# Six tile buffers in the room of the turned ones, masks in two fixed places, and new planning times

## The chip, the cores and the metric

The kernel runs on one core of one Trainium2 chip. The metric is the device time of one execution in microseconds. Time before: 2075.99 us, the median of 3 runs (2071.98 to 2077.3).

## The reference

Two graph layers over N = 3327 nodes with 256 features, all in float32. `adj` is dense in storage, with about 0.5% of its entries above zero.

```python
def _top_p_attention(X, W1, W2, W3):
    q = X @ W1.T @ W2.T
    k = X @ W3.T
    probs = softmax(q @ k.T)
    idx = argsort(-probs)
    sp = take_along_axis(probs, idx)
    cs = cumsum(sp)
    keep_sorted = cs - sp < 0.9
    mask = zeros.at[rows, idx].set(keep_sorted)
    A = probs * mask
    return A / A.sum(-1, keepdims=True)

def layer0(X, S):                       # S = adj, X = relu(layernorm(x))
    R = S + eye(N); R = R / R.sum(-1, keepdims=True)
    Z, Xf, Xa = 0, X, X
    for n in range(2):
        A = _top_p_attention(Xa, W1, W2, W3)
        Xf = R @ Xf
        Xa = A @ Xa
        Z = Z + Xf @ U1[n].T + Xa @ U2[n].T
    return layernorm(X + Z) * ln_g + ln_b

def layer1(h, adj):                     # h = relu(layernorm(x)), 4 heads of 64
    hp = (h @ W).reshape(n, 4, 64)
    s, d = hp . a_src, hp . a_dst
    e = leaky_relu(s[:, :, None] + d[:, None, :], 0.2)
    e = where(adj > 0, e, -inf)
    attn = softmax(e, axis=2)
    return elu(einsum('hij,jhf->ihf', attn, hp))

x = x + layer0(relu(layernorm(x)), adj)
x = x + layer1(relu(layernorm(x)), adj)
```

## The kernel before

Nodes are cut into NT = 26 tiles of 128. The work has three stages. In the two steps of layer 0 (n = 0 and 1 in the code, step 1 and step 2 in the text), each of 26 rows of tiles goes through an attention chain, and each tile also has a full product R @ Xf. Layer 1 then runs over four blocks b of 832 target nodes, with j over the 26 source tiles.

**Who decides the order.** All work is given to a planner (`Plan`, L471 to L583) as pieces: an engine, an estimated length, a rank, the pieces that it needs, and named buffers that it takes and gives back. `order` plays the pieces through in time: whenever an engine is free, it takes the ready piece of lowest rank whose buffers are free. `lag` is the time that the plan lets pass between the end of a piece and the moment when another engine may use its result. The outcome is one fixed order of instructions on each engine. On the chip each engine works its queue in order and waits on semaphores; the plan's times have no other effect than this order. SP (SyncE) issues nearly all DMAs, in one queue.

**A row of attention** (`search` and `attention`, L1463 to L1538). TensorE (PE) makes the logits into `pl` (L906), ScalarE (ACT) exponentiates them into one of the buffers `e` (L921), and ACT and GpSimd (POOL) find a threshold in 2 or 3 evaluations (`count` L958, `step`). VectorE (DVE) takes candidates (`window` L1016 and L1021), sorts, and drops what is below the threshold (`drop` L1072). The row is then transposed: DVE transposes inside 32x32 blocks (`turn_blocks` L1084), SP writes one of three groups to the array `blocks` in HBM (`put_blocks` L1088) and reads it back in the other order in four DMAs (`get_blocks` L1093). PE multiplies its 26 blocks (`attend_blocks` L1100) into the accumulator `acca`, ACT takes the result out (`attended` L1104), and the row's buffer `e` is free. A float32 matmul shows in the profile as two records.

**A full product** (`Full`, L1109, and `full`, L1540). Seven loads of four 128x128 tiles of adj each (256 KB, L1119) go into the buffers `at`; POOL adds the identity to the diagonal tile (`diagonal` L1132); PE multiplies (`some` L1125) into the accumulator `accf`. In step 1 the result is copied to a buffer `f` (`copy` L1136 or `take` L1146), from which DVE adds it (`add`, L1152); in step 2 it is scaled into `main` (L1139 or L1142). Full products are what PE does while rows are not ready. Step 2's need all of step 1's.

**The `stats` of four rows** (L811 to L865): PE makes a product, ACT copies it out of PSUM (`copy` L828), and DVE squares and sums it (L833), ahead of the rows' thresholds.

**Layer 1** (`attend_neighbours`, L1565). For each j two loads (256 and 192 KB, L1680) bring adj's tiles into `at`; ACT makes a mask of zeros and ones from them (Relu L1690, Sign L1691); DVE makes the masked exponents of four heads (L1702, four instructions a j); PE multiplies them (`product` L1718) and sums them (`sums` L1732). The `sums` use the accumulators `acca` and `accf`, so the first of them waits until the last row is `attended`. For j = 0 and 1 of the first block the tiles come into a room of their own (`load_first` L1667) and their masks lie in two places of the scratch buffer `junk` (L1675). The targets' exponents are broadcast from HBM to all partitions once for each block (`broadcast`, L1634). At a block's end the result goes through PSUM, a nonlinearity and the addition of x1, which is fetched into a buffer `f` (L1824), and is stored (L1888).

**Buffers.** The pool `apool` holds `at` (4 of 2 KB a partition), `etpool` holds `et` (3 of 2 KB), used for the masks of layer 1, for the copies of `stats` and for two weights; `f` has 3 buffers of 1056 bytes. The plan counts them as `at=4`, `et=3`, `mask=2`, `f=3` (L867 and L54). Their planning times:

```python
b = plan.put("SP", 0.5, rank - 1.0, row.put_blocks, g, needs=[b], lag=8.0)          # L1527
[plan.put("SP", 0.6, rank - 1.0, row.get_blocks, g, o, needs=[b], lag=5.5) ...]     # L1530
plan.put("SP", 0.4, rank, f.load, q, needs=[after], take=["at"], lag=4.0)           # L1544
full(n, t, (2.0 + 1.3 * t if n == 0 else base + 1.0 + t), ...)                      # L1969
```

`base` is 30 in step 2; row i has the rank base + i, with small offsets for its pieces.

Of the kernel before, what the change touches and what calls it, by code (L numbers as in the profile page):

```python
# [10 lines left out]
F32 = mybir.dt.float32  # L11
BF16 = mybir.dt.bfloat16
# [7 lines left out]
P = 128  # L20
# [5 lines left out]
H = 4  # L26
# [24 lines left out]

REACH = 40.0

BUFS = dict(kk=2, e=4, sc=6, f=3, xa=2, xt=2, kq=3, ystage=2, base=1, mv=4, cum=2)  # L54


@with_exitstack
# [529 lines left out]
def fast(  # L587
# [58 lines left out]
    with ExitStack() as l0:  # L646
        wpool = l0.enter_context(tc.tile_pool(name="wpool", bufs=1))
        small = l0.enter_context(tc.tile_pool(name="small", bufs=2))
        epool = l0.enter_context(tc.tile_pool(name="epool", bufs=4))
        apool = l0.enter_context(tc.tile_pool(name="apool", bufs=4))  # L650
        etpool = l0.enter_context(tc.tile_pool(name="etpool", bufs=3))
        scr = l0.enter_context(tc.tile_pool(name="scr", bufs=1))
        ps_l = l0.enter_context(tc.tile_pool(name="ps_l", bufs=2, space=PSUM))
        ps_a = l0.enter_context(tc.tile_pool(name="ps_a", bufs=1, space=PSUM))
# [20 lines left out]
            GP.memset(gk, 0.0)  # L675
            GP.tensor_copy(gk[:DA, DA + 1 :], ident[:DA, :DA])

        small.tile([P, 8], F32, name="room", bufs=1)
        stat = wpool.tile([P, 2, NT], F32, name="stat")
        sig, zadd, cn, cs = (wpool.tile([P, NT], F32, name=n) for n in ("sig", "zadd", "cn", "cs"))  # L680
        met = wpool.tile([P, 6, NT], F32, name="met")
# [17 lines left out]

        def weights():  # L700
            held = {}
            w1 = etpool.tile([P, 4, P], F32, name="et")
            w1 = w1[:, 0, :].rearrange("p (c o) -> p c o", c=2)
            w2 = small.tile([P, PIECES, 8], F32, name="cands").rearrange("p c r -> p (c r)")[:DA, :DA]
            w1r = small.tile([P, PIECES * 8], F32, name="rest", bufs=1)[:DA].rearrange("p (k o) -> p k o", k=1)
            w1r = [w1r[:, 0, :], small.tile([P, P], F32, name="kq", bufs=BUFS["kq"])[:DA]]
            nc.scalar.dma_start(w1, w1t.rearrange("(c p) o -> p c o", p=P))
            nc.scalar.dma_start(w2, w2t)
            for r in range(2):
                nc.scalar.dma_start(wqk[:, :, r, r * DA : r * DA + DA], w3t.rearrange("(c p) o -> p c o", p=P))  # L710
            for n in range(STEPS):
                cols = slice((1 - n) * D, (2 - n) * D)
                uloads.append(
                    plan.put(
                        "SP", 0.4, -196.5 + n, nc.sync.dma_start, u1[:, :, cols],
                        u1t[n].rearrange("(c p) o -> p c o", p=P), lag=8.0,
                    )
                )

            S.activation(adds[:, 2:], powers[:, :1], AF.Exp)  # L720

            def turn():
                held["ps"] = ps_x.tile([DA, 2, P], F32, name="px")
                for k in range(2):
                    T.transpose(held["ps"][:, k, :], w1[:, k, :], ident)

            def copy():
                for k in range(2):
                    S.copy(w1r[k], held["ps"][:, k, :])

            def product():
                held["ps"] = ps_x.tile([P, 2, DA], F32, name="px")
                for k in range(2):
                    T.matmul(held["ps"][:, k, :], w1r[k], w2, start=True, stop=True)

            def place():
                for r in range(2):
                    S.copy(wqk[:, :, r, (1 - r) * DA : (2 - r) * DA], held["ps"])

            a = plan.put("PE", 0.25, -200.0, turn, take=["px"], needs=[plan.put("", 0.0, -201.0, lambda: None, lag=8.0)])  # L740
            a = plan.put("ACT", 0.5, -200.0, copy, needs=[a], take=["kq"], give=["px"])
            a = plan.put("PE", 0.25, -200.0, product, needs=[a], take=["px"], give=["kq"])
            return plan.put("ACT", 0.5, -200.0, place, needs=[a], give=["px"])
# [8 lines left out]
        def layer1_loads():  # L752

            late = wpool.tile([P, 2 * D + 2 * (H * FH + 2 * H)], F32, name="late")
            g_all, b_all = late[:, :D], late[:, D : 2 * D]
            wa = late[:, 2 * D :].rearrange("p (c o) -> p c o", c=2)
            a_all = etpool.tile([P, H, 2 * FH], F32, name="et")
            nc.sync.dma_start(g_all, ln_g.partition_broadcast(P))
            nc.sync.dma_start(b_all, ln_b.partition_broadcast(P))
            nc.sync.dma_start(a_all, gat_a.partition_broadcast(P))  # L760
            nc.sync.dma_start(wa[:, :, : H * FH], gat_w.rearrange("(c p) o -> p c o", p=P))
            return g_all, b_all, wa, a_all

        def layer1_scores(wa, a_all):

            prod = etpool.tile([P, 2, H, FH], F32, name="et")
            for k in range(2):
                for a in range(2):
                    V.tensor_mul(
                        prod[:, 0],  # L770
                        wa[:, k, : H * FH].rearrange("p (h f) -> p h f", h=H),
                        a_all[:, :, a * FH : (a + 1) * FH],
                    )
                    lo = H * FH + a * H
                    V.tensor_reduce(wa[:, k, lo : lo + H], prod[:, 0], AX.X, ALU.add)

        def moments(n, t, kq, ps_k, ps_g):

# [32 lines left out]
        def stats(n, lo, hi, rank, needs, scaled):  # L811
# [11 lines left out]
                    T.matmul(held["ps"][:, k, :], qg[n, t0 // 4][:, at, :], gks[n], start=True, stop=True)  # L823

            def copy(held, m):
                qg = etpool.tile([P, 4, P], F32, name="et").rearrange("p a b -> p (a b)")
                held["qg"] = qg[:, : 3 * (2 * DA + 1)].rearrange("p (a b) -> p a b", a=3)
                S.copy(held["qg"][:, :m, :], held["ps"][:, :m, :])  # L828

            def square(held, t0, m):  # L830
# [8 lines left out]
            for t0 in range(lo, hi, 2):  # L839
                held, m = {}, min(2, hi - t0)  # L840
                a = plan.put("PE", 0.25 * m, rank, product, held, t0, m, needs=[needs, scaled], take=["px"])
                a = plan.put("ACT", 0.45, rank, copy, held, m, needs=[a], take=["et"], give=["px"])
                ends.append(plan.put("DVE", 0.35 * m + 0.2, rank, square, held, t0, m, needs=[a], give=["et"]))

            def variance():
                V.tensor_mul(cn[:, s], mu, mu)
# [17 lines left out]
            a = plan.put("ACT", 0.6, rank, exps, needs=[a])  # L864
            return plan.put("DVE", 0.6, rank, rest, needs=[a]), ends  # L865

        plan = Plan(dict(rows=1, mvs=3, pl=2, px=2, acca=1, accf=1, et=3, at=4, y=1, e2=2, ec=1, mask=2, e5=1, qg=2, **BUFS))  # L867
        own_e = [[("e", "e5")[i % 5 == 2 - n] for i in range(NT)] for n in range(STEPS)]
        qg = {}

# [649 lines left out]
        def attention(row, rank, total, drops, right):  # L1520
            a = None
            come = []
            for g in range(3):
                b = plan.put(
                    "DVE", 1.17 if g < 2 else 1.44, rank - 1.001, row.turn_blocks, g, needs=[drops[g]]
                )
                b = plan.put("SP", 0.5, rank - 1.0, row.put_blocks, g, needs=[b], lag=8.0)  # L1527
                b = plan.put("", 0.0, -90.0, lambda: None, needs=[b], lag=0.0)
                come.append(
                    [plan.put("SP", 0.6, rank - 1.0, row.get_blocks, g, o, needs=[b], lag=5.5) for o in range(4)]  # L1530
                )
            for j in range(0, NT - 2, 4):
                js = range(j, j + 4 if j < 20 else NT)
# [6 lines left out]
        def full(n, t, rank, right, after):  # L1540

            f = Full(n, t)
            loads = [
                plan.put("SP", 0.4, rank, f.load, q, needs=[after], take=["at"], lag=4.0) for q in range(-(-NT // JC))  # L1544
            ]
            loaded[0] = loads[-1]
            a, own = None, plan.put("POOL", 0.4, -90.0, f.diagonal, needs=[loads[t // JC]])
# [17 lines left out]
        def attend_neighbours(rows, ends, done, fulls):  # L1565
# [80 lines left out]
            for b in range(4):  # L1646
# [9 lines left out]
                def open_den(q=q):  # L1656
                    q["den"] = [ps_a.tile([P, 512], F32, name=n) for n in ("acca", "accf")]

                seen, last_acc, last_den, last_e = [], None, None, None
                group, halves = [], [None, None]  # L1660
                for j in range(NT):
                    rank = r0 + 9.0 * j / NT if b > 0 or j >= 2 else 54.2 + 0.1 * j
# [18 lines left out]
                            at[:, : len(ts), :], adjt[ts[0] : ts[0] + len(ts), :, j, :].rearrange("i p q -> p i q")  # L1681
                        )

                    def mask(held=held, off=off):
                        m = etpool.tile([P, 4, P], F32, name="et").rearrange("p a b -> p (a b)").bitcast(BF16)
                        m = held["mask"] = m[:, :W]
                        A, B = (held.pop(g).rearrange("p i q -> p (i q)") for g in range(2))
                        A, B = A[:, off:], B[:, : W + off - 4 * P]
                        for to, src in ((m[:, : 4 * P - off], A), (m[:, 4 * P - off :], B)):
# [48 lines left out]
                                    tile_position=(0, 32 * k),  # L1738
                                )

                    own = ["et", "mask"]
                    if b == 0 and j < 2:
                        loads, own = plan.put("SP", 0.2, rank, load_first, needs=[opened[0]], lag=4.0), []
                        m_ = plan.put("ACT", 1.8, rank, mask_first, needs=[loads])
                    else:
                        loads = [
                            plan.put("SP", 0.4, rank, load, g, needs=[logits_done], take=["at"], lag=4.0)
                            for g in range(2)
                        ]
                        m_ = plan.put("ACT", 2.2, rank, mask, needs=[loads], take=own, give=["at", "at"])  # L1750
                    mine = ("e", "e", "e", "ec", "e", "e2", "e2")[j % 7]
                    x_ = plan.put(
                        "DVE", 2.0, rank, exponents, 0, needs=[m_, both[0], ends[j][0], dict(ec=opened, e2=more).get(mine),
# [189 lines left out]
        for n in range(STEPS):  # L1943
# [22 lines left out]
            if n == 0:  # L1966
                drawn[0] = rows[-1].pieces["logits"]
            fulls = [
                full(n, t, (2.0 + 1.3 * t if n == 0 else base + 1.0 + t), [p[0] for p in sources], [p[1] for p in sources] if n == 0 else loaded[0])  # L1969
                for t in range(NT)  # L1970
            ]
            done = [attention(r, base + r.i, *found[r.i], right) for r in rows]
# [1 line left out]
            if n == 0:  # L1974
# [21 lines left out]
                def layer1():  # L1996
# [4 lines left out]
                a = plan.put("SP", 1.8, base + NT + 1.0, layer1, needs=[used, stored], take=["et"], lag=8.0)  # L2001
                less = plan.put("POOL", 0.6, base + 5.0, lambda: late["less"](), needs=[a])
                layer1_ready = plan.put(
                    "DVE", 3.7, base + 5.0, lambda: layer1_scores(late["wa"], late["a"]), needs=[a], take=["et"],
                    give=["et", "et"],
                )
                layer1_ready = [layer1_ready, less]
            else:
# [72 lines left out]
```

## Time and profile before

| | |
|---|---|
| median of the runs | 2075.99 us |
| the profiled execution | 2077.04 us |
| its span, first to last instruction | 2075.2 us |
| mean granted TensorE clock | 0.992 |
| VectorE busy | 1696.3 us (82%) |
| ScalarE busy | 1298.7 us (63%) |
| bytes moved by DMA | 361.61 MB, mean 174 GB/s |

The span in 40 slices of 52 us; a digit is the busy share in tenths:

```profile
PE   8999999999999999999999999999998999999997
DVE  5479989887997742888679888898888999999894
ACT  4677685677756405884677777877643456474642
PEclk9999999999999999999999999999999999999999
DMA  3177677776786756687757777676786444444440
```

Step 1 ends near slice 15 (about 780 us), where DVE and ACT nearly stop: step 2's keys need the last row of step 1. Step 2 ends near slice 31 (about 1600 us), and layer 1 follows, where DVE is as full as PE.

The costliest groups of instructions on PE (columns: line, engine, operation, out<-in, shapes, count, busy us, mean ns, idle us before them and what ended it):

```profile
L1100 PE MATMUL acca<-rhs,e 128*128 128x256 f32 x2184 | 485.6, 380 | 4.1 <-DMA e<-blocks 2.3
L1125 PE MATMUL accf<-main,at 128*128 128x257 f32 x1352 | 323.8, 389 | 14.1 <-DMA at<-in_adjt_dram 7.6
L1125 PE MATMUL accf<-c,at 128*128 128x256 f32 x1352 | 308.6, 382 | 5.9 <-DMA at<-in_adjt_dram 2.2
L1718 PE MATMUL pl<-e,main 128*64 128x416 f32 x1024 | 191.6, 517 | 0.0
```

The mean of one is its way through the array; neighbours overlap, so busy time divided by the count is what one costs. The two lines of L1125 are the full products of step 1 and of step 2.

### The profile page before, as it was taken

What the parts mean: (1) busy time and instruction counts of PE and PEld (TensorE: products, weight loads), DVE (VectorE), ACT (ScalarE), POOL (GpSimd) and SP (SyncE); (2) the same over time, 40 slices, a digit from 0 to 9 for tenths busy, and PEclk for the clock granted to TensorE, in tenths of its full rate; (3) what the DMA queues carried; (4) which work ended last, traced back from release to release, by engine and by line L of the source; (5) the groups of instructions that cost most, each with busy time, mean ns of one, the idle gap of its engine ahead of it and who ended that gap; (6) DMA issues with size and microseconds to landing.
All of it is one profiled execution on the core that took longest, in us unless ns stands there. A gap on an engine that the chain in (4) does not pass through costs nothing. (4 is left out here: it accounts for less than half of the span.)

```text
span 2075.2 us, 33982 instructions
## 1 busy us (share of the span) xinstructions
PE 2025.6 (98%) x10519; PEld 1401.3 (68%) x10519; DVE 1696.3 (82%) x3768; ACT 1298.7 (63%) x2630; POOL 1040.1 (50%) x2222
## 2 busy tenths in 40 slices
PE   8999999999999999999999999999998999999997
PEld 6477777878787776788888788778876333333332
DVE  5479989887997742888679888898888999999894
ACT  4677685677756405884677777877643456474642
POOL 5367676665765503787576777878771000000001
PEclk9999999999999999999999999999999999999999
DMA  3177677776786756687757777676786444444440
GB/s 96 38 209 192 188 203 216 194 196 190 198 220 193 209 151 181 199 220 216 196 156 216 202 199 201 192 206 184 214 251 200 117 132 140 140 132 116 117 123 26
DMA packets 637551, 361.61 MB, mean 174 GB/s; under 512 B 373706, under 2 KB 590320, under 8 KB 637360
## 3 DMA queue, kind: packets, MB, share of 16 engines
q1 hardware_dynamic: 636464, 359.13, 61.9%
q8 instruction: 86, 1.41, 0.3%
q14 instruction: 105, 0.86, 0.1%
q10 hardware_dynamic: 896, 0.21, 0.0%
HBM read 254.39 MB, written 104.58 MB: 173 GB/s over the span
## 5 line engine op out<-in xcount | busy, mean ns | idle before, releaser
L1100 PE MATMUL acca<-rhs,e 128*128 128x256 f32 x2184 | 485.6, 380 | 4.1 <-DMA e<-blocks 2.3
L958 ACT ACTIVATE junk<-e,sc 128x3327 fp8e5<-128x3327 f32 x147 | 450.8, 3066 | 39.7 <-POOL sc L995 38.2
L1100 PEld LDWEIGHTS acca<-rhs,e 128*128 128x128 f32 x2184 | 427.9, 197 | 49.4 <-issue 3.5
L1125 PE MATMUL accf<-main,at 128*128 128x257 f32 x1352 | 323.8, 389 | 14.1 <-DMA at<-in_adjt_dram 7.6
L1125 PE MATMUL accf<-c,at 128*128 128x256 f32 x1352 | 308.6, 382 | 5.9 <-DMA at<-in_adjt_dram 2.2
L1125 PEld LDWEIGHTS accf<-main,at 128*128 128x128 f32 x1352 | 253.4, 193 | 76.6 <-issue 19.0
L1125 PEld LDWEIGHTS accf<-c,at 128*128 128x128 f32 x1352 | 252.4, 190 | 57.1 <-issue 8.9
L1021 DVE MAX8 cands<-y 128x8 f32<-128x205 f32 (+1 forms) x832 | 242.7, 362 | 3.7
L1016 DVE SCALAR_TENSOR_TENSOR y<-e,sc 128x1639 f32<-128x1639 f32 x84 | 167.5, 1994 | 65.4 <-POOL sc L1006 64.4
L1881 POOL TENSOR_TENSOR qq<-qq 128x256 f32<-128x256 f32 x4 | 2.9, 730 | 431.6 <-ACT qq L1877 431.5
L1691 ACT ACTIVATE et<-at 128x448 bf16<-128x448 f32 (+1 forms) x204 | 112.2, 550 | 128.6 <-DVE e L1702 73.4
L1718 PE MATMUL pl<-e,main 128*64 128x416 f32 x1024 | 191.6, 517 | 0.0
L921 ACT ACTIVATE e<-pl 128x1024 f32<-128x1024 f32 x126 | 137.8, 1101 | 64.5 <-PE pl L906 54.7
L906 PE MATMUL pl<-kt,qg 64*128 64x512 f32 (+1 forms) x832 | 174.0, 536 | 2.4 <-ACT e L921 2.4
L1084 DVE STREAM_TRANSPOSE e<-e 128x1024 f32<-128x1024 f32 (+1 forms) x126 | 168.7, 1339 | 7.1 <-DVE e L1072 0.5
L1072 DVE SCALAR_TENSOR_TENSOR e<-e,thr 128x1024 f32<-128x1024 f32 (+1 forms) x126 | 170.7, 1354 | 1.5 <-issue 0.4
L1718 PEld LDWEIGHTS pl<-e,main 128*64 128x64 f32 x1024 | 69.3, 137 | 109.8 <-issue 93.7
L1690 ACT ACTIVATE at<-at 128x448 f32<-128x448 f32 (+1 forms) x204 | 110.6, 542 | 45.5 <-DMA at<-in_adjt_dram 45.4
L1702 DVE SCALAR_TENSOR_TENSOR e<-c,low,et 128x832 f32<-128x832 f32 x128 | 129.4, 1071 | 8.1 <-issue 6.2
L906 PEld LDWEIGHTS pl<-kt,qg 64*128 64x128 f32 x832 | 71.4, 186 | 88.3 <-issue 74.1
L1702 DVE SCALAR_TENSOR_TENSOR e<-qq,low,et 128x832 f32<-128x832 f32 x120 | 121.4, 1076 | 8.2 <-ACT at L1690 4.3
L1104 ACT ACTIVATE xa<-acca,sc 128x256 f32<-128x256 f32 x52 | 24.3, 467 | 151.3 <-PE acca L1100 151.2
(547 smaller groups left out, 3454.2 us busy)
## 6 DMA issues: line engine op xcount, KB each, us to landing
at<-in_adjt_dram SPq DMA_DIRECT2D x414, 256.0 KB
blocks<-e SPq DMA_DIRECT2D x84, 512.0 KB
e<-blocks SPq DMA_DIRECT2D x336, 128.0 KB
blocks<-e SPq DMA_DIRECT2D x42, 640.0 KB
e<-blocks SPq DMA_DIRECT2D x168, 160.0 KB
at<-in_adjt_dram SPq DMA_DIRECT2D x102, 192.0 KB
blocks<-qq SPq DMA_DIRECT2D x20, 512.0 KB
qq<-blocks SPq DMA_DIRECT2D x80, 128.0 KB
```

The source lines that it names most:

```text
L906: T.matmul(pl[:, lo : lo + m], qg[self.n, self.i // 4][half, self.i % 4, :], kt[half, 512 * k : 512 * k + m], start=True, stop=True,)
L921: S.activation(to, pl.rearrange("p (g t q) -> p g t q", g=4, t=2), AF.Exp, accum_out=sums[k])
L958: S.activation(junk[:, :N], self.e[:, :N], fn, bias=t, scale=-1.0, accum_out=dst, saturate=False)
L1016: V.scalar_tensor_tensor(self.y[:, : hi - lo], self.e[:, lo:hi], self.up, self.e[:, lo:hi], ALU.is_lt, ALU.mult, accum_out=(self.h0, self. ...
L1021: V.max(self.cands[:, a * PIECES // 2 + k, :], self.y[:, at[k] - lo : at[k + 1] - lo])
L1072: V.scalar_tensor_tensor(piece, piece, self.thr[:, at : at + 1], piece, ALU.is_gt, ALU.mult)
L1084: V.transpose(part, part)
L1100: T.matmul(self.acc, lhs, rhs[self.n][:, j, :], start=(j == 0), stop=(j == NT - 1))
L1125: T.matmul(self.acc[:, : self.w], self.at[j // JC][:, j % JC, :], self.src[:, j, : self.w], start=(j == 0), stop=(j == NT - 1),)
L1691: S.activation(to, src, AF.Sign)
L1702: V.scalar_tensor_tensor(held["e"][:, k, :], extra["both"][b % 2][:, k, :], low[:, j, k : k + 1], held["mask"], ALU.max, ALU.mult,)
L1718: T.matmul(q["acc"][a][k * FH : (k + 1) * FH, c, :C], main[:, j, h * FH : (h + 1) * FH], held["e"][:, h, c * C : (c + 1) * C], start=(j == 0),
```

## The change

`at` gets six buffers. The room comes from `et`, which shrinks from three buffers of 2 KB to one of 3 KB, and from `f`, which shrinks from three to two; an unused tile `room` grows by 32 bytes, so that the sum stays as it was. What had used `et` moves: the copies of `stats` go to `f`; the masks of layer 1 take turns in the two places of `junk` that only j = 0 and 1 had used; the two products of layer 1's weights lie behind `a_all` in the one buffer that is left. Each mask now needs the one before it and takes `mask`, for j = 0 and 1 too. In the plan, a write of blocks counts 7.0 us instead of 8.0, their reads 5.0 instead of 5.5, a tile load of a full product 5.5 instead of 4.0, and the full products of step 2 get the rank base + 2 + 1.05 t instead of base + 1 + t.

```diff
-BUFS = dict(kk=2, e=4, sc=6, f=3, xa=2, xt=2, kq=3, ystage=2, base=1, mv=4, cum=2)
+BUFS = dict(kk=2, e=4, sc=6, f=2, xa=2, xt=2, kq=3, ystage=2, base=1, mv=4, cum=2)
...
-        apool = l0.enter_context(tc.tile_pool(name="apool", bufs=4))
-        etpool = l0.enter_context(tc.tile_pool(name="etpool", bufs=3))
+        apool = l0.enter_context(tc.tile_pool(name="apool", bufs=6))
+        etpool = l0.enter_context(tc.tile_pool(name="etpool", bufs=1))
...
-        small.tile([P, 8], F32, name="room", bufs=1)
+        small.tile([P, 16], F32, name="room", bufs=1)
...
-            a_all = etpool.tile([P, H, 2 * FH], F32, name="et")
+            a_all = etpool.tile([P, 3 * D], F32, name="et")
+            prod = a_all[:, 2 * D :].rearrange("p (h f) -> p h f", h=H)
+            a_all = a_all[:, : 2 * D].rearrange("p (h f) -> p h f", h=H)
...
             def copy(held, m):
-                qg = etpool.tile([P, 4, P], F32, name="et").rearrange("p a b -> p (a b)")
-                held["qg"] = qg[:, : 3 * (2 * DA + 1)].rearrange("p (a b) -> p a b", a=3)
+                qg = small.tile([P, H * FH + 2 * H], F32, name="f", bufs=BUFS["f"])
+                held["qg"] = qg[:, : 2 * (2 * DA + 1)].rearrange("p (a b) -> p a b", a=2)
...
-                a = plan.put("ACT", 0.45, rank, copy, held, m, needs=[a], take=["et"], give=["px"])
-                ends.append(plan.put("DVE", 0.35 * m + 0.2, rank, square, held, t0, m, needs=[a], give=["et"]))
+                a = plan.put("ACT", 0.45, rank, copy, held, m, needs=[a], take=["f"], give=["px"])
+                ends.append(plan.put("DVE", 0.35 * m + 0.2, rank, square, held, t0, m, needs=[a], give=["f"]))
...
-        plan = Plan(dict(rows=1, mvs=3, pl=2, px=2, acca=1, accf=1, et=3, at=4, y=1, ...
+        plan = Plan(dict(rows=1, mvs=3, pl=2, px=2, acca=1, accf=1, et=1, at=6, y=1, ...
...
-                b = plan.put("SP", 0.5, rank - 1.0, row.put_blocks, g, needs=[b], lag=8.0)
+                b = plan.put("SP", 0.5, rank - 1.0, row.put_blocks, g, needs=[b], lag=7.0)
...
-                    [plan.put("SP", 0.6, rank - 1.0, row.get_blocks, g, o, needs=[b], lag=5.5) for o in range(4)]
+                    [plan.put("SP", 0.6, rank - 1.0, row.get_blocks, g, o, needs=[b], lag=5.0) for o in range(4)]
...
-                plan.put("SP", 0.4, rank, f.load, q, needs=[after], take=["at"], lag=4.0) for q in range(-(-NT // JC))
+                plan.put("SP", 0.4, rank, f.load, q, needs=[after], take=["at"], lag=5.5) for q in range(-(-NT // JC))
...
-                    def mask(held=held, off=off):
-                        m = etpool.tile([P, 4, P], F32, name="et").rearrange("p a b -> p (a b)").bitcast(BF16)
-                        m = held["mask"] = m[:, :W]
+                    def mask(j=j, held=held, off=off):
+                        m = held["mask"] = extra["m"][:, j % 2, :]
...
-                    own = ["et", "mask"]
+                    own = ["mask"]
...
-                        m_ = plan.put("ACT", 1.8, rank, mask_first, needs=[loads])
+                        m_ = last_m = plan.put("ACT", 1.8, rank, mask_first, needs=[loads, last_m], take=own)
...
-                        m_ = plan.put("ACT", 2.2, rank, mask, needs=[loads], take=own, give=["at", "at"])
+                        m_ = last_m = plan.put("ACT", 2.2, rank, mask, needs=[loads, last_m], take=own, give=["at", "at"])
...
-                full(n, t, (2.0 + 1.3 * t if n == 0 else base + 1.0 + t), ...
+                full(n, t, (2.0 + 1.3 * t if n == 0 else base + 2.0 + 1.05 * t), ...
```

## The prediction

> **What bounds the kernel now.** I read the engines' totals first, then who TensorE (PE) waited for, then single stretches, then the chain of waits.
>
> ```profile
> PE 2025.6 (98%) x10519; PEld 1401.3 (68%) x10519; DVE 1696.3 (82%) x3768; ACT 1298.7 (63%) x2630; POOL 1040.1 (50%) x2222
> ```
>
> PE is the bound. The change neither adds nor removes a matmul, so it wins or loses only idle PE time and time at a low clock: 2075.2 - 2025.6 = 49.6 us are idle, of which 11.6 lie behind the last matmul block (it ends at 2063.6 in the chain). What PE waited for (total us, times, longest):
>
> ```profile
> PE accf L1125 <- DMA at<-in_adjt_dram: 9.8, 7, 4.2
> PE accf L1125 <- POOL at L1132: 5.5, 3, 2.7
> PE acca L1732 <- ACT xa L1104: 4.5, 1, 4.5
> PE pl L906 <- ACT e L921: 2.4, 2, 1.3
> PE acca L1100 <- DMA e<-blocks: 2.3, 2, 1.4
> ```
>
> The first line is adj's tiles coming late, which more buffers address; the third is one wait at the entry of layer 1. From 1610 to 2040 us PE waits for nothing. Six windows (us, then PE, PEld, DVE, ACT, POOL busy, granted clock, DMA share, GB/s) show these places, each followed by the stretch behind it:
>
> ```profile
> 748.45:753.11 4.66, 2.01 (x8) 1.44 (x8) 0.00 (x0) 0.00 (x0) 0.46 (x1) 1.00 1.07 249
> 753.11:757.00 3.89, 3.89 (x10) 3.19 (x11) 0.00 (x0) 0.00 (x0) 0.00 (x0) 0.56 0.96 238
> 780.00:785.50 5.50, 1.37 (x7) 0.85 (x5) 0.00 (x0) 0.00 (x0) 0.89 (x1) 0.85 0.97 264
> 785.50:791.00 5.50, 5.46 (x14) 4.00 (x16) 0.00 (x0) 0.03 (x1) 0.00 (x0) 0.53 0.45 142
> 1594.00:1599.20 5.20, 0.74 (x6) 0.01 (x2) 1.36 (x2) 2.43 (x6) 0.00 (x0) 1.00 0.60 193
> 1599.27:1602.00 2.73, 2.73 (x20) 1.01 (x24) 2.61 (x5) 2.45 (x5) 1.41 (x2) 0.57 0.61 173
> ```
>
> PE's timeline has waits of 2.66, 4.17 and 4.54 us at the end of the first, third and fifth. Behind each the clock is near half; PE counts as busy there but loses 3.89 x 0.44 = 1.7, 5.5 x 0.47 = 2.6, and 1.7 us (the sixth, with 1602 to 1607 at 0.89).
>
> The chain of waits tells why layer 1's entry waits (start, us, what):
>
> ```profile
> 1585.51 0.48 SPq L1634
> ...
> 1586.60 10.08 DMA at<-in_adjt_dram
> 1596.70 0.64 ACT at L1690
> 1597.37 0.63 ACT et L1691
> ...
> 1598.76 0.47 ACT xa L1104
> ...
> 1599.27 1.30 PE acca L1732 x8
> ```
>
> The second `highs` broadcast (L1634) is issued ahead of a tile load, which then needs 10.08 us. ACT's queue holds that tile's mask ahead of `attended` of the last row (L1104), and PE's `sums` wait for it, though the last attention matmul was over at 1599.27 - 4.54 = 1594.7.
>
> **The change part by part.**
>
> *Six tile buffers, loads planned at 5.5 us.* A tile feeds PE for 1.7 us (36 matmuls of L1125 in 7.79 us, 8 a tile). With four buffers a load leads its use by at most 3 x 1.7 = 5.2 us, with six by 8.7. From SP's issue to the last landing, by the semaphore counts in the trace, loads take 3.8 us in the median and 6.8 at most (the one of the 4.17 us wait): four don't cover that, six do. At the step transition 0.73 + 2.66 + 4.17 = 7.6 us of waits and 1.7 + 2.6 = 4.3 of clock could go, 11.9 in all. What is late next is attention: step 1's last row has its blocks 4.1 us before PE takes them, step 2's first 2.3 us, so without any help from the row chains 4.1 + 2.3 = 6.4 pass through. The chain to step 2's first logits hangs on that last row's matmuls and moves with them. Between 6.4 and 11.9 I take **9.0**. Of the other 2.2 us of tile waits, in step 2, half: **1.1**.
>
> *Entry.* The changed program's issue order, fixed when it is built, has the loads for j = 2 to 5 ahead of the second broadcast, and no mask of a later load ahead of the last `attended`. Up to 4.54 + 1.7 = 6.2 us go; I take **5.2**, leaving a microsecond for what comes next (the stage of the row before, on the same queue).
>
> *Masks in two places.* Masks 2 to 4 had buffers of their own; now mask j's Sign waits for the exponents of j - 2. That is a new wait at the entry: mask 5 stands before the last `attended` on ACT and waits for exponents of j = 2 and 3, 8 x 1.07 = 8.6 us of DVE (L1702), queued just behind the next-to-last row. The cover is the last row's attention, at least 52 x 0.216 = 11.2 us of PE from its first block on, which comes about 14 us after its transposes; so 0. Without cover it costs at most the 4.5 that it had cost before. Later, a tile takes DVE 4 x 1.07 = 4.3 us, and the mask needs 0.63 + 0.45 + 0.47 = 1.6 of them after the wait: cover 2.7, cost 0. The planner held two masks in flight before too (L1691 waits 73.4 us for L1702, PE idle 0).
>
> *Blocks planned shorter (8 to 7, 5.5 to 5.0).* A group's four reads mostly begin 4 to 6 us after its write landed, so the write's microsecond only brings the reads forward. The reads' half microsecond comes out of what is left between their landing and PE: 2 to 6 us in most of 52 rows, but 0.14 in four. Those four lose 0.5 each: **-2.0**. PE's queue is in order, so full products wait behind such a block.
>
> *Full products of step 2 ranked later.* In rows 3 to 7 of step 2 blocks now lie ready for 11 to 23 us while PE does full products, and DVE falls to 36.8 and 37.2 of 50 us (1000 to 1100). PE is full there, so nothing is won directly; the buffers `e` come free earlier and later rows gain cover: **+1.0** of the 1.12 us wait at 1521 and its half clock (1.7).
>
> *`stats` copies in `f`, two instead of three.* They now share with the evacuation of full products. DVE takes the releasing piece first. Waits for `f` are 1.7 + 1.6 = 3.3 us now; from 0 to another 3.3, I take **-0.5**. The x1 fetches in layer 1 have two places as well; SP then waits longer, but tile loads stand 3 masks ahead: 0.
>
> Sum: 9.0 + 1.1 + 5.2 - 2.0 + 1.0 - 0.5 = 13.8 us. The profiled execution took 2077.0 (span 2075.2); 2077.0 - 13.8 = 2063.2. The median of the runs is 1.1 lower, so 2062.1; I say 2063.
>
> **Two rules against the rows.** The Trainium skill's "TensorE: Matmul & The Clock Gate", Part 1, has the clock halve after an idle window of some 3.4 us. The rows above differ: half clock follows a wait of 2.66 us, too, and lasts 3.4 or 6.8. By the rule the 1.7 at 753 would be none of the tiles' doing and the sum 12.1; I keep the row. The rule against this change is in "DMA: Bandwidth & Descriptors", Queues, rings and completion order: SP's copies share one ring per DMA engine and are consumed in order. Tiles and blocks are both on queue q1 here, so two more tiles ahead of a block read, 512 KB at about 264 GB/s, delay it by 1.9 us. The row: a group's reads take about 5.7 us from first issue to last landing in step 1 and step 2 alike. PE consumes no more tiles per us than before, so I count bursts only, within the 2.0 above; the rule is the slow rival.
>
> **Rivals.**
> - *The gain is handed to the rows.* PE comes earlier and waits for blocks. For it: 0.1 to 4 us of cover in most rows of step 2. Against: 20 us of cover in rows 3 to 7 and the later rank. Left are 2.3 at the transition and 2.5 at the entry: 2072.
> - *Block reads late behind tiles (slower).* Each read comes 1.9 later and 0.5 is planned away. 17 rows have less than 2.4 us of cover; their shortfalls sum to 20.5 us. Even if 9 us of the gains stay: 2077.0 + 20.5 - 9 = 2088.5. It decides from some 1.2 us of delay. Against it: each stall gives the next row cover.
> - *Six buffers aren't used*: other waits keep SP behind and loads are issued no earlier. SP waits 201 us for PE to free tiles at L1119, which speaks against it. Then 2074.
>
> **Numbers.** Forecast 0.55 (its own range 2053 to 2069), handed to rows 0.19, late reads 0.19, unused 0.07. A change under 0.3% (6.2 us) can't be told from none. Faster: the forecast's and 0.03 of the second, 0.58; same: the rest of the second and most of the last, 0.21; slower 0.21. For 8 in 10 the range goes from 2051 (whole gains) to 2085.
>
> **What would show it.** PE's waits for adj's tiles under 2 us and no half clock between 740 and 800; no wait of `sums` for L1104; L1100's waits for blocks under 5 us. Wrong if these grow past 10, or if PE waits for L1702 in layer 1.

## The result, and the profile after

| | before | after |
|---|---|---|
| median | 2071.65 us (18 runs, 2069.05 to 2077.30) | 2070.20 us (18 runs, 2068.22 to 2072.94) |
| profiled execution, span | 2077.04, 2075.2 us | 2071.44, 2069.6 us |
| ratio of the times | | 0.9990 (95%: 0.9982 to 0.9997) |

A tenth of a per cent faster, where 13.8 us were forecast. The profiled execution of before lay 5.4 us above the median of its 18 runs, so the sum also began too high. From the median it would have ended at 2071.65 - 13.8 = 2057.9 us, and 12.3 us are missing.

PE's totals after, from the page, and then the list of what PE waited for (total us, times, longest):

```profile
PE 2022.4 (98%) x10519; PEld 1400.2 (68%) x10519; DVE 1695.1 (82%) x3754; ACT 1300.4 (63%) x2644; POOL 1036.0 (50%) x2222
```

```profile
PE acca L1102 <- DMA e<-blocks: 9.2, 5, 5.7
PE pl L1719 <- DVE e L1703: 4.9, 1, 4.9
PE accf L1127 <- DVE main L1144: 4.3, 6, 1.0
```

(Lines move by two up to about L1690, and by one behind: L1100 is now L1102, L1718 is L1719.) The waits for adj's tiles, 9.8 us before, and the 4.5 us wait for the last `attended` have left the list. In their place stand waits for blocks (2.3 before) and one wait of layer 1's first products for DVE's exponents.

Two stretches show where time came from and where it went. First before, then after (PE, PEld, DVE, ACT, POOL busy with counts, granted clock, DMA share, GB/s):

```profile
740.00:800.00 60.00, 52.20 (x219) 40.88 (x218) 14.05 (x56) 7.91 (x22) 5.25 (x9) 0.91 0.61 173
1535.00:1580.00 45.00, 43.23 (x202) 33.84 (x201) 42.76 (x93) 10.07 (x22) 19.87 (x28) 1.00 0.81 231
```

```profile
740.00:800.00 60.00, 59.53 (x280) 47.82 (x279) 16.39 (x72) 23.22 (x48) 11.32 (x25) 1.00 0.63 187
1535.00:1580.00 45.00, 32.84 (x141) 24.27 (x140) 37.37 (x90) 12.24 (x29) 16.10 (x21) 0.87 0.75 215
```

At the step transition PE now works 59.53 of 60 us at the full clock. At the end of step 2 it does 141 matmul records where before did 202. Counting PE's records from the start by such windows gives the lead: 6946 against 6877 by 1535 us, 69 records of 0.22 us (L1102: 486.4 us for 2184), or **15 us**; by 1580 us 7087 against 7079, or **2 us**. (Estimates: records of other lines are longer or shorter.) Of the 69, 8 are there by 740 us and all by 800. The gain was there, and it was lost in 45 us. The rows tell the same: step 2's first row starts on PE at 841.5 us (857.8 before), the next-to-last at 1535.9 (1551.7), the last at 1579.5 (1579.7).

What happens there, on three engines of the kernel after. DVE's timeline (start, us, engine, line, operation, out<-in, shapes, count):

```profile
1527.42 8.24 DVE L1703 SCALAR_TENSOR_TENSOR e<-qq,low,junk 128x832 f32<-128x832 f32 x8
1535.59 2.38 DVE L1018 SCALAR_TENSOR_TENSOR y<-e,sc 128x1639 f32<-128x1639 f32 x1
```

SP's timeline, and two lines of the kernel before, where the broadcast (L1636, there L1634) stands behind the last row's reads (L1095, there L1093). First after, then before:

```profile
1564.18 0.55 SPq L1090 DMA_DIRECT2D blocks<-e  x1
1564.78 2.37 SPq L1682 DMA_DIRECT2D at<-in_adjt_dram  x2
1567.19 1.25 SPq L1636 DMA_DIRECT2D c<-highs  x2
1568.48 10.67 SPq L1095 DMA_DIRECT2D e<-blocks  x8
```

```profile
1580.70 2.94 SPq L1093 DMA_DIRECT2D e<-blocks  x4
1585.51 0.99 SPq L1634 DMA_DIRECT2D c<-highs  x2
```

PE's timeline, with the wait in brackets, and a window around it:

```profile
1569.80 4.03 PE L1719 MATMUL pl<-e,main 128*64 128x416 f32 x8 [4.89 <-DVE e L1703]
1579.55 5.89 PE L1102 MATMUL acca<-rhs,e 128*128 128x256 f32 x13 [5.71 <-DMA e<-blocks]
```

```profile
1568.60:1585.70 17.10, 10.18 (x23) 6.22 (x24) 8.06 (x8) 3.93 (x8) 3.00 (x3) 0.50 0.97 269
```

DVE makes all eight exponents of j = 0 and 1 in one piece before it turns to the last row's `window`; before, those of j = 0 came in two halves (at 1542.44 and 1550.24 us), one of them behind the `window`'s first part, and those of j = 1 behind the row's transposes. SP issues the last row's third write, two tile loads of layer 1, and then the second broadcast of `highs`, ahead of that row's block reads. A broadcast is two transfers of 832 KB. The first group's reads land 10.9 us after their issue, where the median of the rows is 5.7 and the last row of before took 7.2. PE waits 4.89 and 5.71 us, and the clock is at half for 17.1 us.

### The profile page after: what moved, and what is told of

Same layout as the page of the kernel before. It is cut to its first block, busy times and chain, and to the rows that moved or that the text cites. A ratio compares the mean times of both kernels' runs of the same rounds, so it can differ in the third digit from the quotient of the medians.

```text
span 2069.6 us, 34036 instructions
## 1 busy us (share of the span) xinstructions
PE 2022.4 (98%) x10519; PEld 1400.2 (68%) x10519; DVE 1695.1 (82%) x3754; ACT 1300.4 (63%) x2644; POOL 1036.0 (50%) x2222
## 5 line engine op out<-in xcount | busy, mean ns | idle before, releaser
L1102 PE MATMUL acca<-rhs,e 128*128 128x256 f32 x2184 | 486.4, 381 | 9.2 <-DMA e<-blocks 9.2
L1102 PEld LDWEIGHTS acca<-rhs,e 128*128 128x128 f32 x2184 | 428.5, 197 | 58.7 <-issue 12.0
L1127 PE MATMUL accf<-main,at 128*128 128x257 f32 x1352 | 317.9, 385 | 7.4 <-ACT f L1138 2.6
L1692 ACT ACTIVATE junk<-at 128x448 bf16<-128x448 f32 (+1 forms) x204 | 112.2, 550 | 188.0 <-DVE e L1703 122.2
L1719 PE MATMUL pl<-e,main 128*64 128x416 f32 x1024 | 194.2, 520 | 4.9 <-DVE e L1703 4.9
L1703 DVE SCALAR_TENSOR_TENSOR e<-qq,low,junk 128x832 f32<-128x832 f32 x128 | 129.5, 1076 | 23.0 <-PE acca L1102 17.6
L1719 PEld LDWEIGHTS pl<-e,main 128*64 128x64 f32 x1024 | 70.0, 137 | 115.7 <-issue 94.4
L1703 DVE SCALAR_TENSOR_TENSOR e<-c,low,junk 128x832 f32<-128x832 f32 x128 | 129.4, 1072 | 7.9 <-issue 3.7
L1102 PE MATMUL acca<-rhs,qq 128*128 128x256 f32 x520 | 114.7, 380 | 0.0
```

The source lines that it names most:

```text
L1102: T.matmul(self.acc, lhs, rhs[self.n][:, j, :], start=(j == 0), stop=(j == NT - 1))
L1127: T.matmul(self.acc[:, : self.w], self.at[j // JC][:, j % JC, :], self.src[:, j, : self.w], start=(j == 0), stop=(j == NT - 1),)
L1703: V.scalar_tensor_tensor(held["e"][:, k, :], extra["both"][b % 2][:, k, :], low[:, j, k : k + 1], held["mask"], ALU.max, ALU.mult,)
L1719: T.matmul(q["acc"][a][k * FH : (k + 1) * FH, c, :C], main[:, j, h * FH : (h + 1) * FH], held["e"][:, h, c * C : (c + 1) * C], start=(j == 0),
```

## The experiments

My theory after the traces: the lead is real, and the end of step 2 gives it back, through SP's queue and DVE's order. The rivals: the two kernels never differed by the waits of one profile; or the shorter plan eats the gain row by row; or the rooms bring nothing.

| kernel | what it is | median us (runs) | ratio to before (95%) |
|---|---|---|---|
| hold_broadcast | after, second broadcast held | 2061.09 (5) | 0.9954 (0.9941 to 0.9968) |
| exponents_later | after, first exponents held | 2055.93 (5) | 0.9930 (0.9917 to 0.9944) |
| before_end_mended | before, both held | 2065.00 (11) | 0.9969 (0.9958 to 0.9979) |
| rooms_alone | after, the plan of before | 2070.98 (13) | 1.0005 (0.9997 to 1.0013) |
| rooms_end_mended | rooms_alone, both broadcasts and the exponents held | 2069.77 (14) | 0.9991 (0.9981 to 1.0001) |
| plan_alone | before, the plan of after | 2094.43 (5) | 1.0119 (1.0099 to 1.0138) |
| rank_back | exponents_later, rank of before | 2067.23 (22) | 0.9979 (0.9972 to 0.9985) |
| blocks_longer | exponents_later, blocks' times of before | 2048.93 (5) | 0.9891 (0.9876 to 0.9907) |
| loads_shorter | exponents_later, loads' time of before | 2060.38 (6) | 0.9950 (0.9934 to 0.9966) |
| both_broadcasts_held | exponents_later, both broadcasts held | 2054.82 (6) | 0.9919 (0.9905 to 0.9932) |

Each ratio is to runs of the kernel before that were taken with those of its row. Their medians were 2071.65 us for the kernel after, 2070.17 for hold_broadcast, exponents_later and rooms_alone, 2071.99 for rooms_end_mended, before_end_mended and plan_alone, and 2072.75 for the rest. So a difference of medians from two of these groups can be off by up to 2.6 us; the difference by the ratios then stands beside it.

**Was the first profile of before a chance?** The kernel before, profiled again.

> The kernel before, a second profile. Lead given back at the end: the tile waits at 753 and 785 us (2.66 and 4.17 us) and the half clock behind them are there again, since they belong to four buffers; the wait of sums for the last attended (4.54) too. Rival, a slow profile: if the waits for adj's tiles sum to under 4 us here (9.8 in the first profile), most of the 9.0 us was never there to win, and the two kernels differ by little for that reason alone.

2073.3 us, a single execution. The waits for tiles are there again, 9.6 us, with 2.66 and 3.84 at the transition and half clock behind both; the wait for the last `attended` is 3.8. That rival falls.

**SP's queue.** All edits of this part add only needs at the end of step 2; the order before about 1500 us is that of the kernel they start from. Each row keeps its reads as `row.pieces["come"]`, and the turning of its last blocks as `row.pieces["turned"]`.

```diff
-got, after = [], [spread[: b + 1], opened[b % 2], used_heads[b % 2]]
+got, after = [], [spread[: b + 1], opened[b % 2], used_heads[b % 2], rows[-1].pieces["come"] if b == 1 else None]
```

> The changed kernel, with the second broadcast of highs held back until the last row's block reads are issued. If the DMA queue costs the end (1.7 MB ahead of the reads, about 6.5 us at 264 GB/s): the reads land some 6 us earlier, PE's wait of 5.71 us for the last row's blocks falls under 1, some 3 us of half clock go with it, and the median falls from 2070 to 2061 to 2064. If DVE's order is the cause (8.24 us of exponents ahead of the last row's window): the row's transposes are as late as before, the wait of 4.89 us stays, and the median moves by less than 3 us.

2061.09 us, 9.1 below the kernel after (7.5 by the ratios), as the queue's theory had it. The wait of 4.89 us for DVE is still there; the wait of 5.71 us for the last row's blocks has become one of 0.36, and the reads of its first group land 6.5 us after issue:

```profile
1570.96 9.31 PE L1102 MATMUL acca<-rhs,e 128*128 128x256 f32 x39 [0.36 <-DMA e<-blocks]
```

The half clock lasts 6.8 us instead of 17.1. The instructions of PE (10519 records), DVE, ACT and POOL come in the same order in both kernels from first to last; only SP's order differs. So the transfers ahead of the reads are shown to cost the larger part.

**DVE's order.** Here the exponents alone are held; with that the planner puts the second broadcast behind the reads without being told.

```diff
-logits_done, last_e], take=[mine], hold=1.95,
+logits_done, last_e, rows[-1].pieces["turned"] if b == 0 and j >= 0 else None], take=[mine], hold=1.95,
```

> The changed kernel, with layer 1's first exponents held until the last row's blocks are turned (the planner then puts the second broadcast behind the last row's reads by itself). DVE's order: the last row's window starts 8.2 us earlier, its blocks land before PE comes to them, neither 4.89 nor 5.71 us of waiting is left nor the 17.1 us of half clock, up to 19 us in all; the median falls to 2052 to 2060. DMA queue alone: as with the broadcast held, 2061 to 2064. If the exponents are then late for PE, a new wait for L1703 takes their place and the median stays above 2066.

2055.93 us. The last row starts on PE at 1564.7 us instead of 1579.5. The same window as above, of this kernel:

```profile
1535.00:1580.00 45.00, 44.91 (x215) 34.09 (x217) 42.92 (x88) 12.05 (x29) 13.64 (x19) 0.98 0.88 240
```

PE is full (44.91 of 45 us), with 215 records where the kernel after had 141. Against the broadcast held alone DVE's order is worth 2061.09 - 2055.93 = 5.2 us. Together the end had cost 2070.20 - 2055.93 = 14.3 us (12.4 by the ratios to before, 0.9990 and 0.9930). The split into 9.1 and 5.2 holds for this order of the two mends: the exponents held with the broadcast kept ahead of the reads were not run.

**The same holds in the kernel before**, second broadcast and exponents:

> The kernel before with the holds of the second broadcast and of layer 1's first exponents. If the gain of the tile rooms is real and only the end gives it back: the kernel before can win no more than its own wait at the entry (3.8 to 4.5 us) and the half clock behind it, so 2064 to 2068, some 8 to 12 us above the changed kernel with the same holds (2055.9). If the holds alone make the time and the rooms bring nothing: 2054 to 2058 here as well.

2065.00 us: before's own end was worth 6 to 7 us, and with both ends mended the change is worth 2065.00 - 2055.93 = **9.1 us** (8.1 by the ratios). The waits for tiles are still there (13.1 us). So the rooms with their plan do bring something, and the holds alone don't make the time.

**The rooms without the new plan.** Here the planned times and the rank of before come back:

```diff
-row.put_blocks, ..., lag=7.0)    row.get_blocks, ..., lag=5.0)    f.load, ..., lag=5.5)    base + 2.0 + 1.05 * t
+row.put_blocks, ..., lag=8.0)    row.get_blocks, ..., lag=5.5)    f.load, ..., lag=4.0)    base + 1.0 + t
```

> The changed kernel with the planned times of loads and blocks (8.0, 5.5, 4.0 us) and the rank of step 2's full products put back: the new rooms alone. If the rooms carry the gain and the new plan's end gives it back: under 2062. If the shorter and longer plans matter too (rows have less or more cover): between 2064 and 2075. If the rooms bring nothing by themselves: 2071 as before.

2070.98 us, no gain, and yet PE is further ahead by 1535 us than in the kernel after: 6986 records, a lead over before of 109 or 24 us. PE's timeline shows where it goes:

```profile
1531.48 1.89 PE L1127 MATMUL accf<-c,at 128*128 128x256 f32 x8
1555.55 3.75 PE L1102 MATMUL acca<-rhs,e 128*128 128x256 f32 x8 [22.18 <-DMA e<-blocks]
```

One wait of 22.18 us, in the next-to-last row, with the clock at half from 1537.5 to 1561.4 (and not from 1555 to 1571, as the next expectation has it). SP had issued layer 1's first tile loads and both broadcasts ahead of that row's reads, and the first group's took 14.9 us to land:

```profile
1540.28 9.09 SPq L1095 DMA_DIRECT2D e<-blocks  x4
```

I took the queue for the whole cause and held both broadcasts and the exponents:

> The new rooms with the old planned times and rank (the kernel that took 2071.0, with one wait of 22.2 us for blocks at the next-to-last row), and three holds at its end: the first broadcast of highs behind the next-to-last row's reads, the second behind the last row's, layer 1's first exponents behind the last row's turned blocks. If the broadcasts ahead of the reads made that wait: it goes, and most of the half clock behind it (1555 to 1571 us) with it, some 22 + 8 us; the median falls to 2041 to 2048, below every other kernel. If the row's blocks were late for another reason (its puts or DVE's order): the wait stays over 10 us and the median over 2058.

2069.77 us: the expectation failed, and the kernel before with its end mended took 2065.00 beside it. The PE timeline:

```profile
1532.62 1.89 PE L1127 MATMUL accf<-c,at 128*128 128x256 f32 x8
1545.97 3.75 PE L1102 MATMUL acca<-rhs,e 128*128 128x256 f32 x8 [11.46 <-DMA e<-blocks]
1571.38 8.58 PE L1719 MATMUL pl<-e,main 128*64 128x416 f32 x32 [10.31 <-DVE e L1703]
```

The queue was only half of the wait: 22.18 became 11.46. The first line is the last full product, done at 1534.5 us. Behind it PE has nothing but the last two rows, each bound by its own chain on DVE, POOL and SP, and with the exponents held not even layer 1. A lead won by doing full products sooner is worthless here: PE arrives early at two rows that are no earlier. The wait of 10.31 us comes from the hold itself, so what the rooms alone would bring with another end stays open.

**The parts of the plan**, each put back alone in the kernel with the exponents held (2055.93).

```diff
+full(n, t, (2.0 + 1.3 * t if n == 0 else base + 1.0 + t), ...      # rank_back
+row.put_blocks, ..., lag=8.0)   row.get_blocks, ..., lag=5.5)      # blocks_longer
+f.load, ..., lag=4.0)                                              # loads_shorter
```

> The changed kernel with the first exponents held (2055.9), and the rank of step 2's full products put back to the earlier one. As forecast, the rank is worth 1.0 us: 2056 to 2058. Rival from the rooms alone with a mended end (full products all done by 1534 us, then waits of 11.46 and 10.31 us with nothing else for PE to do): the later rank is what keeps work for the last rows, PE waits 10 to 20 us in all beside the last two rows, 2063 to 2072.

2067.23 us, 11.3 slower (10.1 by the ratios): the rival holds. One wait for blocks of 12.7 us and one of 3.0 for exponents stand at the end:

```profile
PE acca L1102 <- DMA e<-blocks: 12.7, 1, 12.7
```

PE's last full product is done at 1536.1 us; with the later rank full products last until 1557.8. The later rank keeps them for the last rows.

> The changed kernel with the first exponents held (2055.9), and the blocks' planned times put back to 8.0 and 5.5 us. As forecast, the shorter plan costs 2.0 us through rows with no cover: 2053 to 2055. If the short plan gains by bringing rows forward: 2057 to 2062. Waits for blocks 1 us or less in rows 26 to 49 in both cases.

2048.93 us, 7.0 faster (8.1 by the ratios), faster than the kernels before and after, and the fastest of all here. The shorter plan costs, and more than forecast. It did take the rows' cover: by the semaphore counts, rows with a group of blocks that lands less than 2.4 us before PE takes it are 17 of 52 before, 31 after, 28 with the exponents held, and 15 here. But PE's waits for blocks fall only from 3.0 to 1.7 us. Between the two profiled executions (6.5 us) PE's busy time falls by 4.0 us, from 2019.0 to 2015.0 with the same number of records. So little of the gain is waits for blocks, and where it comes from, these runs don't settle.

> The changed kernel with the first exponents held (2055.9), and the loads' planned time put back from 5.5 to 4.0 us. If six places alone cover the loads (8.7 us of lead against 6.8 at most): waits for adj's tiles stay under 1 us and the median lies within 2 us of 2055.9. If the longer plan is needed for it: waits for tiles over 3 us and 2059 to 2063.

2060.38 us, 4.5 slower (4.1 by the ratios), but PE waits for tiles for 0.2 us in all. So neither story of the expectation fits. The six places do cover the loads; the planned time acts by moving the order (PE's is another from 105 us on), and which part of it costs is not shown. Its last row starts at 1570.3 us (1564.7).

> The kernel before with only the new planned times (7.0, 5.0, 5.5 us) and the later rank, four tile buffers, no new rooms. If the plan is worth something by itself: under 2066. If it costs by itself what the rooms then win (rows have a microsecond or two less of cover, by two traces), and four buffers can't use loads planned longer: the waits for adj's tiles stay near 9 us or grow, waits for blocks grow, 2074 to 2090. Within 2069 to 2073 it does nothing.

2094.43 us. With four buffers the new plan costs 22 us. The waits for tiles grow to 20.6. Rooms alone nothing, plan alone 22 us lost, both together, with a mended end, 8 to 9 won: the parts don't add up.

**The first broadcast**, held behind the next-to-last row's reads as well:

> The changed kernel with layer 1's first exponents held (2055.9) and both broadcasts of highs behind block reads, the first behind the next-to-last row's. If the first broadcast delays the next-to-last row as the second delayed the last: PE's waits for blocks fall from 3.0 us to about 1, 2053 to 2055. If that row's wait isn't of the queue: 2056 again; above 2058 if the first broadcast then comes late for layer 1's exponents.

2054.82 us against 2055.93 (intervals overlap), with waits for blocks of 3.0 us in both: not told apart.

## Why the prediction was wrong

**The step that failed is *Entry*.** It read from the order of issue that the second broadcast now stands behind the loads of j = 2 to 5 and that no mask stands before the last `attended`. Both are so, and that wait is gone. But it left "a microsecond for what comes next", and did not look for the last row's reads in the same list: they stand behind the broadcast. What came next cost 12 to 14 us: 7.5 to 9.1 by the transfers ahead of the reads, and 5.2 by DVE's order, which the step did not look at either.

With 1.66 MB of broadcast issued ahead of them the last row's reads took 10.9 us to land; with the broadcast behind them 6.5. The mechanism had been named, as the slow rival: the Trainium skill's "DMA: Bandwidth & Descriptors" (Queues, rings and completion order) has SP's copies share one ring on each DMA engine, consumed in order. It was then priced with two tiles, 512 KB or 1.9 us, on every read. The rows agree with the rule but not with that price: over the first 49 rows the median from a group's first read to its landing is 5.7 us before and after. It bit at one place, through a broadcast worth an estimated 6.3 us at the same 264 GB/s, of which the reads show 10.9 - 5.7 = 5.2.

**Six buffers** (9.0 + 1.1): right in mechanism, and small in size. No wait for tiles is left, and the transition alone gives 7.3 us of PE time and, with a clock of 1.00 for 0.91, the forecast's 4.3 us of clock: 11.6 of the 11.9 that it held possible, by the first profile of before. "What is late next" was not attention in general: the lead passed untouched through step 2 up to its next-to-last row.

**Entry's gain** (5.2): near in size for what it named, by the kernel before with its end mended (6 to 7 us), though the holds there are other edits.

**Blocks shorter** (-2.0): right in sign, 7 to 8 measured, and mostly not through the waits for blocks that it counted. **Rank** (+1.0): right in sign, 10 to 11 measured, and the reason was wrong. It was argued from cover for later rows; its worth is the work that it leaves for the last ones. The sum without the entry, 9.0 + 1.1 - 2.0 + 1.0 - 0.5 = 8.6, lies close to the 8.1 to 9.1 measured, but two of its terms were off by some 5 and 10 us in opposite directions, so the agreement is partly luck.

**Masks in two places** (0): right. ACT's waits for the exponents in `e` grow from 73.4 to 122.2 us, and PE's list has none that follows from it in layer 1 proper. The one wait for L1703 is that of the first products, queued behind rows. **`stats` in `f`** (-0.5): not tried by itself; PE's waits for `f` come to 2.6 + 2.4 = 5.0 us, where they were 3.3.

The forecast's signs of failure were the right ones: waits for L1102 were to stay under 5 us and came to 9.2, and PE was not to wait for L1703. The time fell near that of "handed to the rows", but not by its mechanism: one row took nearly all.

## What to carry to other kernels

A lead on the bounding engine is worth what the next fixed point lets through: before pricing a gain, follow it to the end of the stage, and list in order of issue what stands ahead of that stage's last transfers, large prefetches of the next stage above all. Keep work that needs nothing (here the full products) for the end of a stage whose last pieces are bound by a chain. Edits to a planner's times act through the whole order; here rooms and plan were worth 0 and -22 us alone and +8 to +9 together, so price them together, and measure them in a kernel whose end is mended.

## What the runs showed of the hardware

The half clock outlasts the waits: in the kernel after it ran 17.1 us around waits of 4.89 and 5.71, until 6.1 us behind the second, and cost half of 10.18 us of PE work. The stretches seen while PE had work were 3.4, 6.8, 10.2, 13.7, 17.1 and 23.9 us long.

It begins in fixed steps. In the first profiled execution of the kernel before the stretches at half clock begin at 12.45, 97.79, 753.15, 783.87, 1521.14 and 1599.65 us, which lie whole multiples of 3.413 us apart. The steps lie elsewhere in each execution, and so the same wait does not always have half clock behind it. The wait of 2.66 us at the step transition had it in both profiled executions of the kernel before. In that of before_end_mended, whose order is the same up to there, the wait of 2.66 us ends at 749.24 us and the granted clock is 1.00 from 745 to 752. So the 1.7 us of clock that the forecast counted behind this wait come or not with where it falls.

Two executions of the same work differ by it. The kernel after and the one with the broadcast held have the same instructions in the first 100 us. First after, then the other:

```profile
0.00:100.00 100.00, 89.98 (x382) 54.13 (x383) 49.54 (x183) 57.92 (x150) 41.74 (x134) 0.97 0.25 72
```

```profile
0.00:100.00 100.00, 90.44 (x395) 54.23 (x396) 51.07 (x192) 59.32 (x151) 42.51 (x136) 1.00 0.25 73
```

Two stretches of 3.4 us at half clock (0.97 in the mean) are in the first and not in the second, which by then is 13 records ahead. That is some 3 us between executions of the same work, twice the 1.45 us between the medians of before and after.
